# A fused decoder layer: when the second output projection begins, and where the down weights are split

## The chip, the cores and the metric

The kernel runs on one core of one Trainium2 chip. The metric is the device time of one execution in microseconds (us); lower is better. The core has five engines that run beside each other, each through its own list of instructions in a fixed order: TensorE (matmuls; PE in the profile, PEld for its weight loads), VectorE (DVE), ScalarE (ACT), GpSimd (POOL) and SyncE (SP, which here issues nearly all DMA transfers). An engine that waits for one instruction's inputs holds up all that stands behind it in its list.

## The reference

Two batches of 512 tokens of width 1024 go through one decoder layer with LayerNorm after each of three parts:

```python
x = layernorm(x + attn(x, wq, wk, wv, wo))        # 32 query heads, 8 key/value heads of 128,
                                                  # causal, window of 128 tokens
x = layernorm(x + matmul(fake_quant(x), fake_quant(ctx)))   # ctx: (2, 1024, 1024), 8-bit levels
x = layernorm(x + ffn(x, w_gate, w_up, w_down))   # silu(gate) * up, 2752 wide; both the inner
                                                  # values and the result are truncated to int8 steps
```

All inputs are float32. The truncations make the result depend on exact values, so the kernel keeps float32 precision where they lie.

## The kernel before, in words

Projections are computed with Strassen's scheme in the form with seven products: a product of a 2x2 block matrix takes seven block matmuls in place of eight, and sums of blocks on both sides are formed on VectorE. `strassen` (L119 to L174) emits the seven products of one weight tile, each of four matmuls into a PSUM bank, and yields after each. Its bank reads (L141 and L152 on ScalarE, L144, L155, L158, L161, L166, L169, L172 on VectorE) form the four blocks of the result.

**Attention** (`attention`) goes through 16 groups: eight key/value heads for each batch. For each group it projects keys, values and queries, and runs scores, softmax and the weighted sum (`scores`, `transpose_p`, `weigh`) in four blocks of 128 tokens. The sums of the attention output that the output projection needs are formed by `keep` and written to DRAM (`kept`, L422), seven slots for each group. The projections of a group are pieces of the group before; so in the last group of batch 1 (g = 7) there is no projection left to lie beside the softmax.

**The output projection** (`project_out`, L462 to L577) is a generator for each batch. It has 56 steps: seven products `k`, in the order of `grow`, times eight groups `g`. A step loads a right block of `wo` (or its precomputed sums) into `or`, a left tile `ol` from `kept`, forms sums of the right block on VectorE (`ot`, L500 to L505) and does seven matmuls (L560) into four PSUM banks `y`. After the eighth group of each product, `read(k)` (L532, L533) adds the banks into the residual tile `xres`. After products 5 and 3 two halves of the tokens are complete.

**The context part** (`Cross`): `context(b)` loads eight blocks of ctx (`raw`), quantises each with three VectorE operations (L612 to L618) and one on ScalarE, and sums columns with matmuls. `tokens(b)` takes a tile of 128 tokens through LayerNorm, quantise, transpose, matmul with the context (`m`, L683), LayerNorm again, and transpose into `x2T`, the input of the feed-forward part. Batch 0's tiles are written to DRAM (`spill`), as both batches use the same `xres` tile.

**The feed-forward part** (`feed_forward`) has 22 units for each batch: 21 of 128 rows of gate and up weights with `strassen`, and a rest of 64 rows. `activate` forms the inner values on ScalarE and VectorE. The down weights of a unit are loaded to `wd` (`load_down`, one buffer) and split into a high part `hi` (ScalarE, L762) and a low part `lo` (VectorE, L763) by `split`, so that two matmuls of a faster type give float32 accuracy. Every few units `down` (matmuls at L806) adds partial sums into `acc`. While batch 0's units run, the output projection, context and tokens of batch 1 are stepped in between.

**What sets the order.** The generators are stepped by three queues (`Background`). `behind` holds the context of batch 0 and both output projections; `aside` holds the tokens of batch 0, and then context and tokens of batch 1; `ahead` prepares weight sums. `in_attention` steps `behind` at each call and one other queue when the step was not a `LUMP`; `in_feed_forward` steps `aside` and `behind` once after each of the seven products of a unit. On top of this, the tile layer orders each engine's instructions by its own plan of when inputs are ready, so it may put an instruction ahead of others emitted earlier. `keep_in_program_order` marks an instruction that keeps its place in the emitted order on its engine. The order that comes out is fixed when the program is built.

Of the kernel before, what the change touches and what calls it, by code (L numbers as in the profile page):

```python
# [9 lines left out]
F32 = mybir.dt.float32  # L10
# [4 lines left out]
ALU = mybir.AluOpType  # L15
# [3 lines left out]
P = 128  # L19
# [3 lines left out]
D = 1024  # L23
# [155 lines left out]
class Background:  # L179
# [6 lines left out]
    def add(self, steps, share=1):  # L186

        self.queue.append([steps, share, 0])
# [273 lines left out]
def project_out(nc, tc, b, xres, spaces, psum, kept, complete, wo_d, sums, x_d, gap):  # L462
# [45 lines left out]
    while b and (b - 1, "tokens") not in complete:  # L508
        yield
# [5 lines left out]
    x = respool.tile([P, TPB, D], F32, tag="xres", name=f"xres{b}")  # L515
    for i in range(TPB):
        nc.sync.dma_start(out=x[:, i], in_=x_d[ts(b * TPB + i, P), :])
        xres[b * TPB + i] = x[:, i]
    yield
# [8 lines left out]
    def read(k):  # L528
        w = stream.tile([P, 4, HQ], F32, tag="right", name=f"yw_{b}_{k}")
        p1, u4, u2, u3 = (w[:, j] for j in range(4))  # L530
        q1, q6, q7, q5 = banks[0][:, 0], banks[0][:, 1], banks[1][:, 0], banks[3][:, 1]
        add = lambda out, in0, in1: nc.vector.tensor_tensor(out, in0, in1, ALU.add)  # L532
        nc.scalar.copy(p1, q1)  # L533
        tc.keep_in_program_order(add(u2, q6, p1))
        add(u3, q7, u2)
        add(u4, q5, u2)
        rows = w[:, 0:2], u3.unsqueeze(1).to_broadcast([P, 2, HQ])
        grown = banks[2], banks[3]
        to = [[x[:, 2 * h + q, ts(e, HALF)].rearrange("p (e c) -> p e c", e=2) for q in range(2)] for h, e in grow[k][1]]
        if len(to) == 1:  # L540
            for q in range(2):
                add(to[0][q], grown[q], to[0][q])
            for q in range(2):
                add(to[0][q], rows[q], to[0][q])
        else:
            whole = w[:, 0:2], w[:, 2:4]
            for q in range(2):
                add(whole[q], grown[q], rows[q])
            for block in to:
                for q in range(2):  # L550
                    add(block[q], whole[q], block[q])

    for n, (k, g) in enumerate(steps):
        while n + 2 < len(steps) and (b, steps[n + 2][1], "kept") not in complete:
            yield
        left, mine, sums_now = lefts.pop(n), factors.pop(n), following
# [15 lines left out]
        if g == LAST:  # L572
            read(k)
            if k in (5, 3):
                complete.add((b, 1 if k == 5 else 0))
            for j in range(gap):
                yield None if j else LUMP  # L577
# [137 lines left out]
def feed_forward(nc, tc, ident, xres, spill, x2T, xbuf, tpool, wpool, left, right, gate_up, wd_d, pools, stream, ps_y, out, between, finish_between):  # L715

    one_pool, raw_pool, b_work, ps_p = pools
    with ExitStack() as ctx:
# [18 lines left out]
        def load_down(u):  # L737
            m = units[u][1]
# [6 lines left out]
        def split(u):  # L745
# [16 lines left out]
            nc.scalar.copy(hi, raw[u])  # L762
            nc.vector.tensor_tensor(lo, raw[u], hi.bitcast(F32), ALU.subtract)  # L763
            halves[u] = (hi, lo)

# [73 lines left out]
        def finish(t, x, sums=None):  # L839

            if sums is None:
                sums = [acc[t]]
                a = wdp.tile([P, D], F32, tag="wd", name=f"fin_{t}", bufs=1)
# [53 lines left out]
        for u, (b, m) in enumerate(units):  # L897
            load_unit(u + 1)
            if m == NCHUNK:
                load_down(u)  # L900
            if m == NCHUNK:
                if b == 0:
                    finish_between()
                    right[1] = strassen_right(nc, tpool, x2T[1], "t2_1")
                rest_unit(u, b)
            else:
                g, up = gate_up_tiles(u)
                outs = g[:, :NH], g[:, NH:], up[:, :NH], up[:, NH:]
                for k, _ in enumerate(strassen(nc, (ps_p, ps_y if b else ps_p), work, left.pop(u), right[b], outs, u)):
# [4 lines left out]
                    if k == 1:  # L914
                        load_down(u)
                    between(k)
# [3 lines left out]
            split(u)  # L920
# [40 lines left out]
def decoder_layer(ctx, tc, x, xT, ctx_kv, wq, wk, wv, wo, s1, z1, s2, z2, wgu, wgu_rest, wd, out):  # L961
# [52 lines left out]
    def output(b):  # L1014
        return project_out(nc, tc, b, xres, (resid, stream), ps_y, kept[b], complete, wo, wo_sums, x, 2)
# [118 lines left out]

    aside.add(cross.context(1), 2)
# [52 lines left out]
```

## Time and profile before

| | us |
|---|---|
| median of three runs | 1926.13 |
| lowest, highest | 1924.7, 1931.46 |
| the profiled execution | 1926.28 |
| its span, first to last instruction | 1924.6 |
| PE busy in the span | 1879.7 |
| VectorE busy | 1369.9 |
| ScalarE busy | 562.5 |

The mean granted clock of TensorE over the span is 0.995 of full speed. The trace holds start and end of each instruction, what released it, and each DMA's issue and landing. Line numbers (L12) are those of the kernel before; tiles are named as in the program, without buffer numbers. In a row "1.66 <-ACT s L348" says that the engine stood idle for 1.66 us before the row's first instruction, and that it was released by ScalarE's instruction on tile `s` at L348. A float32 matmul shows as two records. In time on the span, attention of both batches takes 0 to about 1018 us, the feed-forward units of batch 0 about 1000 to 1550, those of batch 1 to about 1875, and the last sums, LayerNorms and output writes the rest.

### The profile page before, as it was taken

How to read it: one execution, taken by the hardware profiler on the slowest of the kernel's cores; microseconds unless marked ns; L12 is line 12 of the kernel's file. 1: busy time of each engine (PE TensorE's matmuls, PEld its weight loads, DVE VectorE, ACT ScalarE, POOL GpSimd, SP SyncE). 2: the span in 40 equal slices, each digit the busy share in tenths (PEclk: the TensorE clock that was granted, in tenths of full speed). 3: DMA queues.
4: the chain of work that ended last, by engine and by line, in shares of the span. 5: the costliest groups of instructions: out<-in, count | busy, mean ns of one | idle time of the engine just before them, and what ended most of it. 6: DMA issues, size and time to landing. Idle time of an engine off the chain costs nothing.

```text
span 1924.6 us, 24642 instructions
## 1 busy us (share of the span) xinstructions
PE 1879.7 (98%) x8666; PEld 1549.5 (81%) x8678; DVE 1369.9 (71%) x3021; ACT 562.5 (29%) x1569; POOL 13.7 (1%) x32
## 2 busy tenths in 40 slices
PE   9999999999999999999989999999999999999997
PEld 6888888888888888888767878888877778888885
DVE  4678888787767776777787876556778697555657
ACT  1333343333122122123452221111223354221224
POOL 0000000000000000000000000000000000000000
PEclk9999999999999999999989999999999999999999
DMA  8578788778798778855448765566653245543421
GB/s 306 176 264 288 275 279 281 259 258 265 242 328 269 264 273 294 279 171 199 154 169 317 274 226 188 206 225 205 211 193 119 83 168 188 185 169 119 150 97 44
DMA packets 183323, 416.88 MB, mean 217 GB/s; under 512 B 16672, under 2 KB 93728, under 8 KB 183200
## 3 DMA queue, kind: packets, MB, share of 16 engines
q1 hardware_dynamic: 181760, 412.94, 62.1%
q10 hardware_dynamic: 1440, 2.36, 0.3%
q8 instruction: 69, 1.13, 0.2%
q14 instruction: 54, 0.44, 0.1%
HBM read 318.77 MB, written 96.47 MB: 216 GB/s over the span
## 4 chain that ended last, share of the span: by engine, by line
PE 44%; DVE 9%; DMA 6%; ACT 3%; issue 1%; SPq 0%; DVEq 0%; ACTq 0%
PE prod L132 23%; PE y L560 11%; PE d L806 6%; DMA wd<-in_wd_dram 4%; DVE lo L763 1%; PE ps L336 1%; ACT hi L762 1%; PE m L683 1%; PE o L395 1%; PE o L396 1%; DMA raw<-in_ctx_dram 1%; PE x L692 0%; DVE halves L763 0%; PE rest L798 0%; PE pt L372 0%
## 5 line engine op out<-in xcount | busy, mean ns | idle before, releaser
L560 PE MATMUL y<-or,ol 128*128 128x256 f32 x896 | 246.4, 379 | 0.0
L560 PEld LDWEIGHTS y<-or,ol 128*128 128x128 f32 x896 | 168.9, 190 | 24.3 <-issue 1.0
L560 PE MATMUL y<-ot,ol 128*128 128x256 f32 x672 | 184.5, 383 | 3.9 <-DVE ot L501 3.2
L132 PE MATMUL prod<-xT,w 128*128 128x256 f32 x752 | 184.2, 381 | 0.2
L132 PE MATMUL prod<-t,w 128*128 128x256 f32 x752 | 177.2, 379 | 0.1
L132 PE MATMUL prod<-t,s 128*128 128x256 f32 x752 | 177.1, 379 | 0.1
L132 PE MATMUL prod<-x2T,wgu 128*128 128x256 f32 x672 | 162.5, 382 | 2.0 <-ACT st L141 2.0
L132 PEld LDWEIGHTS prod<-xT,w 128*128 128x128 f32 x752 | 139.6, 190 | 26.9 <-issue 9.6
L132 PEld LDWEIGHTS prod<-t,w 128*128 128x128 f32 x752 | 140.1, 190 | 24.3 <-issue 7.7
L132 PEld LDWEIGHTS prod<-t,s 128*128 128x128 f32 x752 | 140.3, 190 | 23.7 <-issue 5.3
L132 PE MATMUL prod<-t,wgu 128*128 128x256 f32 x672 | 157.3, 379 | 1.3 <-DVE st L144 1.3
L132 PE MATMUL prod<-t,sgu 128*128 128x256 f32 x672 | 156.9, 380 | 0.8 <-ACT x2T L693 0.8
L560 PEld LDWEIGHTS y<-ot,ol 128*128 128x128 f32 x672 | 125.1, 190 | 29.1 <-DVE ot L501 10.5
L132 PEld LDWEIGHTS prod<-x2T,wgu 128*128 128x128 f32 x672 | 128.2, 191 | 21.3 <-ACT st L141 2.8
L132 PEld LDWEIGHTS prod<-t,wgu 128*128 128x128 f32 x672 | 127.2, 190 | 20.3 <-DVE st L144 2.2
L132 PEld LDWEIGHTS prod<-t,sgu 128*128 128x128 f32 x672 | 126.9, 190 | 19.5 <-ACT x2T L693 1.6
L806 PE MATMUL d<-hi,act 128*128 128x512 f32 x256 | 108.1, 422 | 1.8 <-DMA or<-in_wo_dram 1.5
L360 ACT ACTIVATE s<-s,top 128x128 f32<-128x128 f32 x256 | 99.5, 390 | 33.8 <-DVE top L357 32.8
L346 ACT COPY s<-ps 128x128 f32<-128x128 f32 x192 | 39.6, 232 | 223.3 <-PE ps L336 223.3
L806 PE MATMUL d<-lo,act 128*128 128x512 f32 x256 | 101.1, 395 | 0.0
L820 DVE TENSOR_TENSOR acc<-d,acc 128x512 f32<-128x512 f32 x104 | 71.4, 690 | 41.3 <-PE d L806 40.8
L155 DVE TENSOR_TENSOR st<-prod,st 128x256 f32<-128x256 f32 x89 | 37.5, 422 | 84.2 <-PE prod L132 84.1
(210 smaller groups left out, 2985.8 us busy)
## 6 DMA issues: line engine op xcount, KB each, us to landing
kept<-factors SPq DMA_DIRECT2D x112, 448.0 KB, 3.6
ol<-kept SPq DMA_DIRECT2D x112, 448.0 KB, 5.1
w<-in_wq_dram SPq DMA_DIRECT2D x64, 512.0 KB, 4.4
or<-wo_sums SPq DMA_DIRECT2D x64, 512.0 KB, 5.1
sgu<-sums SPq DMA_DIRECT2D x42, 768.0 KB, 5.7
or<-in_wo_dram SPq DMA_DIRECT2D x48, 512.0 KB, 4.5
wgu<-in_wgu_dram SPq DMA_DIRECT2D x42, 512.0 KB, 4.2
wd<-in_wd_dram SPq DMA_DIRECT2D x42, 512.0 KB, 4.3
```

The source lines that it names most:

```text
L132: nc.tensor.matmul(ps, left[k - 1][:, c, :], right[k - 1][:, c, :], start=start and c == 0, stop=c == KH - 1, skip_group_check=True)
L155: nc.vector.tensor_tensor(u3, two, p1, ALU.add)
L336: nc.tensor.matmul(ps[:, k, cut // BLOCK : G + 1].rearrange("p d w -> p (d w)"), qT[b, g][:, G * i + c].rearrange("p h w -> p (h w)"), kT[ ...
L346: nc.scalar.copy(s[:, c, c * BLOCK :], ps[:, k, : G - c].rearrange("p d w -> p (d w)"))
L360: nc.scalar.activation(s[:, h, :], s[:, h, :], AF.Exp, bias=top[:, h : h + 1], scale=QSCALE, accum_out=total[:, h : h + 1],)
L395: nc.tensor.matmul(ps, v[b, g][:, i - 1, :], both, start=True, stop=False)
L396: nc.tensor.matmul(ps, vd[b, g][:, i - 1, :], cur, start=False, stop=True)
L560: nc.tensor.matmul(banks[bank][:, half], left[:, SLOT[j]], mine[j], start=grow[k][0] and g == 0 and half == 0, stop=g == LAST, skip_group_ ...
L683: nc.tensor.matmul(ps, a1T[:, c, :], a2[c][:, half], start=c == 0, stop=c == KC - 1)
L762: nc.scalar.copy(hi, raw[u])
L806: nc.tensor.matmul(ps, act[:, ts(i, P)], half[:, part], start=start and k == 0, stop=stop and k == len(parts) - 1)
L820: nc.vector.tensor_tensor(acc[t][:, ts(e, HALF)], ps, acc[t][:, ts(e, HALF)], ALU.add)
```

## The change

It has five parts.

1. The projection of batch 1 no longer waits at its beginning for the tokens of batch 0. It loads its first right and left tiles, then waits until the last group of attention has begun (`begun`, which is `last_group`). The tile `xres` of batch 1 is allocated and loaded at step 4 (`NKV - 4`), and only there does it wait for the tokens of batch 0.
2. `read(k)` is a generator: it forms all row sums first (`whole`), yields `LUMP`, adds the first block into `xres`, yields `LUMP` again, and adds the rest. The last add of each pair's first keeps its program order. The two yields that followed the read (`gap`) are gone.
3. The context of batch 1 is put behind 28 empty steps in `aside`, four units of seven.
4. For the units of batch 1, the down weight of the next unit is loaded after the fourth product of a unit (`k == 3`), and the split of the present one is made in two halves at fixed places: `hi` after the second product (`k == 1`), `lo` after the third (`k == 2`), both kept in program order. Before, load and split were emitted in the same unit and could be moved by the tile layer.
5. The working tile `fin` of the finish of batch 0's tokens moves from the tag `wd` to the tag `base`.

```diff
-def project_out(nc, tc, b, xres, spaces, psum, kept, complete, wo_d, sums, x_d, gap):
+def project_out(nc, tc, b, xres, spaces, psum, kept, complete, wo_d, sums, x_d, begun):
...
-    while b and (b - 1, "tokens") not in complete:
-        yield
     for n in range(3):
         load_right(n)
         if n < 2:
             load_left(n)
     yield
-    x = respool.tile([P, TPB, D], F32, tag="xres", name=f"xres{b}")
-    for i in range(TPB):
-        nc.sync.dma_start(out=x[:, i], in_=x_d[ts(b * TPB + i, P), :])
-        xres[b * TPB + i] = x[:, i]
-    yield
+    while b and not begun[0]:
+        yield
     following = right_sums(0)
...
-        to = [[x[:, 2 * h + q, ts(e, HALF)].rearrange("p (e c) -> p e c", e=2) for q in range(2)] for h, e in grow[k][1]]
-        if len(to) == 1:
+        whole = w[:, 0:2], w[:, 2:4]
+        for q in range(2):
+            add(whole[q], grown[q], rows[q])
+        yield LUMP
+        for n, (h, e) in enumerate(grow[k][1]):
             for q in range(2):
-                add(to[0][q], grown[q], to[0][q])
-            for q in range(2):
-                add(to[0][q], rows[q], to[0][q])
-        else:
-            whole = w[:, 0:2], w[:, 2:4]
-            for q in range(2):
-                add(whole[q], grown[q], rows[q])
-            for block in to:
-                for q in range(2):
-                    add(block[q], whole[q], block[q])
+                block = x[:, 2 * h + q, ts(e, HALF)].rearrange("p (e c) -> p e c", e=2)
+                last = add(block, whole[q], block)
+                if q == 0:
+                    tc.keep_in_program_order(last)
+            if n == 0:
+                yield LUMP
...
+        if n == NKV - 4:
+            while b and (b - 1, "tokens") not in complete:
+                yield
+            x = respool.tile([P, TPB, D], F32, tag="xres", name=f"xres{b}")
+            for i in range(TPB):
+                nc.sync.dma_start(out=x[:, i], in_=x_d[ts(b * TPB + i, P), :])
+                xres[b * TPB + i] = x[:, i]
...
         if g == LAST:
-            read(k)
+            yield from read(k)
             if k in (5, 3):
                 complete.add((b, 1 if k == 5 else 0))
-            for j in range(gap):
-                yield None if j else LUMP
...
         def load_down(u):
+            if u == len(units):
+                return
...
-            nc.scalar.copy(hi, raw[u])
-            nc.vector.tensor_tensor(lo, raw[u], hi.bitcast(F32), ALU.subtract)
+            first = nc.scalar.copy(hi, raw[u])
+            if u >= PER:
+                tc.keep_in_program_order(first)
             halves[u] = (hi, lo)
+
+        def rest_of_split(u):
+            hi, lo = halves[u]
+            last = nc.vector.tensor_tensor(lo, raw[u], hi.bitcast(F32), ALU.subtract)
+            if u >= PER:
+                tc.keep_in_program_order(last)
...
-                a = wdp.tile([P, D], F32, tag="wd", name=f"fin_{t}", bufs=1)
+                a = one_pool.tile([P, D], F32, tag="base", name=f"fin_{t}")
...
             if m == NCHUNK:
-                load_down(u)
-            if m == NCHUNK:
                 if b == 0:
+                    load_down(u)
                     finish_between()
                     right[1] = strassen_right(nc, tpool, x2T[1], "t2_1")
+                else:
+                    split(u)
+                    rest_of_split(u)
                 rest_unit(u, b)
...
-                    if k == 1:
+
+                    if b == 0 and k == 1:
                         load_down(u)
+                    elif b and k == 1:
+                        split(u)
+                    elif b and k == 2:
+                        rest_of_split(u)
+                    elif b and k == 3:
+                        load_down(u + 1)
                     between(k)
...
-            split(u)
+            if b == 0:
+                split(u)
+                rest_of_split(u)
+                if m == NCHUNK:
+                    load_down(u + 1)
...
+    aside.add(iter([None] * 28))
     aside.add(cross.context(1), 2)
     aside.add(cross_tokens(1))
```

More of the change, by code (lines that the diff above doesn't have):

```diff
@@ L1014, in output @@
     def output(b):
-        return project_out(nc, tc, b, xres, (resid, stream), ps_y, kept[b], complete, wo, wo_sums, x, 2)
+        return project_out(nc, tc, b, xres, (resid, stream), ps_y, kept[b], complete, wo, wo_sums, x, last_group)
     def cross_tokens(b):
```

## The prediction

> **What bounds the kernel now.** I read the page first, then busy time by stretch, then what TensorE waited for, then order and chain in the stretches that stand out.
>
> ```profile
> PE 1879.7 (98%) x8666; PEld 1549.5 (81%) x8678; DVE 1369.9 (71%) x3021; ACT 562.5 (29%) x1569; POOL 13.7 (1%) x32
> ```
>
> TensorE (PE) is the bound; nothing in the change removes one of its instructions, so all that can change is time in which it waits or runs slowly. By stretch (columns: length, busy us and count of PE, PEld, DVE, ACT, POOL, then granted clock, DMA share, GB/s):
>
> ```profile
> 970.00:985.00 15.00, 13.16 (x73) 10.11 (x73) 12.28 (x32) 12.78 (x38) 0.00 (x0) 1.00 0.49 160
> 985.00:1000.00 15.00, 10.65 (x45) 6.97 (x43) 12.41 (x28) 8.35 (x26) 0.00 (x0) 0.75 0.54 211
> 1000.00:1030.00 30.00, 28.09 (x115) 21.20 (x114) 19.83 (x46) 7.72 (x28) 0.00 (x0) 0.96 0.76 285
> 1030.00:1150.00 120.00, 116.19 (x525) 97.25 (x525) 93.74 (x185) 28.52 (x38) 0.00 (x0) 1.00 0.74 262
> 1150.00:1375.00 225.00, 225.00 (x1028) 192.94 (x1027) 139.37 (x291) 32.75 (x57) 0.00 (x0) 1.00 0.63 215
> 1375.00:1600.00 225.00, 219.06 (x995) 172.44 (x998) 178.27 (x370) 86.49 (x131) 1.94 (x3) 1.00 0.42 145
> 1600.00:1825.00 225.00, 219.24 (x991) 186.59 (x991) 133.06 (x226) 58.33 (x92) 0.95 (x1) 1.00 0.46 160
> ```
>
> Idle PE: 1.8+4.4+1.9 = 8.1 us from 970 to 1030 (end of attention, start of the feed-forward), 3.8 from 1030 to 1150, none from 1150 to 1375, 5.9 from 1375 to 1600 (tokens of batch 1 beside the feed-forward), 5.8 from 1600 to 1825 (second half of the feed-forward). These 23.6 us are what the change can reach. The order of PE's work in the first:
>
> ```profile
> 984.71 1.67 PE L683 MATMUL m<-a,a1T 128*128 128x512 bf16 x7 [1.66 <-ACT s L348]
> 993.00 1.44 PE L336 MATMUL ps<-kT,qT 128*128 128x160 f32 x4 [2.56 <-DVE s L350]
> 998.29 1.97 PE L692 MATMUL x<-ident,xres 128*128 128x128 f32 x8 [1.51 <-DVE xres L85]
> 1000.08 3.21 PE L132 MATMUL prod<-x2T,wgu 128*128 128x256 f32 x8
> ```
>
> PE waits for the last token tile of batch 0 (quantise, context product, LayerNorm, transpose) and for the last softmaxes, and there is nothing else in its order. It also slows: eight product records take 3.21 us here against 1.89 at 940 us, and the five groups from 993 to 1003 lose 0.73+0.49+0.70+0.94+1.32 = 4.2 us against the same groups elsewhere.
>
> What ended PE's waits, and in the last stretch the chain behind it:
>
> ```profile
> PE prod L132 <- DVE u L158: 5.8, 6, 1.4
> PE y L560 <- DVE ot L501: 3.2, 5, 1.7
> PE ps L336 <- DVE s L350: 3.2, 3, 2.6
> PE prod L132 <- ACT st L141: 2.0, 2, 1.5
> ...
> 1635.49 7.52 DMA wd<-in_wd_dram
> 1643.02 0.02 issue
> 1643.04 1.05 ACT hi L762
> 1644.10 0.02 issue
> 1644.12 1.22 DVE lo L763
> ```
>
> VectorE stands at a `lo` whose down weight has not landed, and behind it is the read of the product bank (L158) that PE needs. All six waits of 5.8 us lie between 1597 and 1809.
>
> **The change part by part.** The sum is against the profiled execution, 1926.3 us (span 1924.6); the median of three is 1926.1, the same.
>
> *Second output projection from the last group on.* In the changed kernel's instruction order 35 projection matmuls of batch 1 (all of the first five steps) stand ahead of the first feed-forward product; before, 10 do. A matmul is two records, eight records take 1.73 us, so one is 0.43 us and the 25 give 10.8 us of work in the hole; two attention products (four records of 0.43 us, 1.7 us) also come before it. Against this the chain grows. The context product `m` ends about 2.3 us later, as projections stand between its parts; the 20 further right sums on VectorE (0.34 us each start to start, 6.8 us) fall mostly into its 5.3 us of idle and the 2.3 us in which it waits for the square root (994.3 to 996.6). Followed by hand, x's transposes come at 1001.3 instead of 998.3 and the first product ends at 1006.6 instead of 1003.1: 10.8+1.7-3.5 = 9.0 us gained. One wait is new: step 7 of the projection now stands right behind the last attention product (about 1018), and needs factors of the last group that are written to DRAM (issued near 1010; the same write landed after 7.1 us before, beside four loads of x) and read back (4 to 5 us when quiet, 9 at the worst row): 1015 to 1023. I take 3 us there (0 to 6), and 1 us back from the slow matmuls. Hole: -7 us (-11 to 0).
>
> The row with the clock at 0.75 has no single wait over 2.56 us. The Trainium skill (TensorE: Matmul & The Clock Gate, Part 1) has the clock drop after an idle window of about 3.4 us; by that no wait here is long enough and the slow matmuls might stay in the changed kernel too, and the sum would be some 1 us less gain. The row shows the drop without such a wait, so I go by the row.
>
> *x of batch 1 loaded at step 4.* Four loads that wait for the spill of the last tile. SP stands 4.4 us for it (998.27 to 1002.69) in both; now projection loads for steps 4 to 8 are ahead of it in SP's order instead of behind, and only the last group's factor writes and step 7's load queue behind. That is the wait priced above.
>
> *Context put off by 28 steps.* Its eight blocks cost VectorE 0.81+0.69+0.69 = 2.2 us each, 17.5 us, and eight 512 KB loads. They go from 1010-1125 (VectorE 78% busy, 262 GB/s, 3.8 us of PE idle) to about 1110-1240 (62%, 215 GB/s, no idle). There SP passes weight and projection loads first. One block's late load (7.6 us to landing at 1116.9) made the 1.7 us wait at 1125; it can come again at another place. The lumps of the first read, in parts, stand between the activation's steps. Together -2.5 us (-4 to +2).
>
> *Read in parts.* Same count of VectorE operations: eleven for the first product, seven for the others. For single blocks the product banks are now read after the row sum instead of before it: about 0.3+3x0.42 = 1.6 us later on that bank, covered by two yields, each with four product matmuls (1.7 us). In attention it touches at most the 3.2 us of waits for `ot`: 0 (-2 to +2).
>
> *Tokens of batch 1.* Their order moves. From `m` to x's transposes VectorE and ScalarE need 9.9 us in the trace (988.4 to 998.3). In the new order the cover is 9.5 us or more for three tiles and 5.9 us for the last; between transpose and context product nine product matmuls stand for that tile where two stood. Of 5.9 idle and some 6 us of late issue I take -4 us (-8 to +4).
>
> *Split bound, weight loaded a unit ahead.* For batch 1, 22 units each have one ScalarE copy (1.05 us) and one VectorE subtraction (1.22 us) at a fixed place, in the first and second product of the unit, behind this order: `st` copy, `hi`, then the previous unit's magnitude. A unit is 28 matmuls, 12.1 us. The load goes out when `lo` ends, about 6 us into the unit, lands 3.1 to 7.5 us later (rows of this stretch), at 9 to 13.5, and is wanted at 14.4 (12.1 plus the first product). So the 5.8 us of waits behind `lo` go. Next late: the previous activation, 1.2 us longer. From L172 to its end took 6.1 us, so it ends 8.2 us into a unit where the bank read L155 is due at 8.7: 0.5 us spare, another 0.8 before PE stands. At the partial sums (one in four units) up to 0.5 us. -5 us (-6.5 to +3). `fin` moved to the `base` tile: its last readers are the tokens, done before; nothing waits.
>
> Sum: -7 -2.5 +0 -4 -5 = -18.5; 1926.3-18.5 = 1907.8, say **1908 us**. The tail after 1875 is unchanged.
>
> **The rivals.**
> *The wait only moves (not faster).* Step 7's factors come at 1023 or later, the softmax chain slips by the same, and the tokens give nothing: 0 -2.5 +0 +0 -5: 1918.8. For it: DMA at 285 GB/s after 1000, landings of 7 to 9 us there. Against: PE's order before step 7 has 4 us of attention waits of its own that hide part.
> The Trainium skill (DMA: Bandwidth & Descriptors, "Two DMAs through the same engine are not ordered") has the issuing engine wait for a write's semaphore before a read of the same bytes; that speaks against moving step 7 forward. Rows agree: loads of `ol` behind factor writes.
>
> *ScalarE stands at the bound copy (slower).* If a down weight lands later than 8.4 us after its issue, every unit of batch 1 loses the difference, as `hi` has a fixed place before the magnitude and the bank copies. With the other parts at -13.5 us, 20 units must lose 1.2 us each to reach +10: landing at 9.6 us, 1936 us. For it: all five loads of a unit now come in one burst. Against: the longest landing in this stretch is 7.5 us, a unit asks for 2.3 MB in 12.1 us, 190 GB/s.
>
> *All of it (faster yet).* Hole -11, context -4, tokens -8, splits -6.5: 1897.
>
> That the change is not made by the scheduler doesn't hold: the new order shows the moved matmuls and one split per unit.
>
> **How the numbers follow.** Forecast 0.62 (its own range 1901 to 1916), all of it 0.10, wait moves 0.16, ScalarE 0.12. Range 1896 to 1922: it reaches past 1897 and 1918.8 and leaves out the slower case. 0.5% is 9.6 us, about what a measurement of this kernel can tell from no change: faster 0.72, same 0.16, slower 0.12.
>
> **What would show it.** Right: PE over 13.5 of 15 us in the stretch before the first product with the clock near 1; the wait for `u` L158 under 1 us in total; no PE wait for a DMA over 3 us. Wrong: a PE wait for `ol` at step 7; ScalarE waiting for `wd` with PE idle behind it in batch 1; waits for `ot` or `st` grown between 1050 and 1550.

## The result, and the profile after

The changed kernel takes 1911.2 us (median of six runs, 1909.64 to 1915.19) against 1929.66 us for the kernel before on the same chip (1924.7 to 1931.99): ratio 0.991, 95% interval 0.9892 to 0.9929. The profiled execution took 1913.13 us with a span of 1911.1 us. The two profiled spans differ by 13.5 us and the medians by 18.5 us, because the profiled run of before (1926.28 us) is among its shorter ones and that of after among its longer ones. What follows accounts for the 13.5 us of the traces.

The page's line of engines, and busy time by stretch (columns: length, busy us and count of PE, PEld, DVE, ACT, POOL, then granted clock, DMA share, GB/s):

```profile
PE 1873.8 (98%) x8667; PEld 1552.2 (81%) x8678; DVE 1370.0 (72%) x3021; ACT 563.2 (29%) x1571; POOL 13.7 (1%) x32
```

```profile
970.00:985.00 15.00, 13.89 (x74) 10.47 (x73) 13.10 (x33) 9.19 (x28) 0.00 (x0) 1.00 0.71 231
985.00:1000.00 15.00, 12.17 (x51) 9.42 (x50) 12.96 (x34) 4.68 (x15) 0.00 (x0) 0.89 0.77 271
1000.00:1030.00 30.00, 27.96 (x127) 21.20 (x126) 20.49 (x43) 10.86 (x38) 0.00 (x0) 1.00 0.77 280
1030.00:1150.00 120.00, 119.40 (x543) 101.72 (x542) 85.09 (x169) 24.73 (x38) 0.00 (x0) 1.00 0.73 253
1150.00:1375.00 225.00, 222.68 (x1013) 189.41 (x1013) 152.56 (x316) 39.49 (x64) 0.00 (x0) 1.00 0.65 223
1375.00:1600.00 225.00, 216.09 (x982) 171.97 (x984) 174.69 (x361) 90.55 (x133) 1.93 (x3) 0.99 0.42 141
1600.00:1825.00 225.00, 224.55 (x1022) 193.36 (x1022) 129.70 (x223) 51.94 (x88) 0.00 (x0) 1.00 0.45 154
```

Set beside the same rows of before: the stretch from 985 to 1000 holds 51 matmul records in place of 45 and a clock of 0.89 in place of 0.75; from 1030 to 1150 PE is almost full (119.40 for 116.19); from 1150 to 1375 it has become less full (222.68 for 225.00), and so it has from 1375 to 1600 (216.09 for 219.06); from 1600 to 1825 it is full (224.55 for 219.24). The change wins in three places and loses in two. What PE waited for:

```profile
PE y L561 <- DMA ol<-kept: 4.1, 2, 2.8
PE x L691 <- DVE xres L85: 3.9, 1, 3.9
...
PE y L561 <- DVE ot L501: 2.9, 5, 1.6
```

The 5.8 us behind the bank read `u` L158 are gone. The two longest entries are new: a load of the projection that comes late, and the LayerNorm of batch 1's tokens.

Busy time alone misses what PE loses by running slowly, so I also took, for each matmul record of TensorE, the time from its start to the next matmul's start less the median of that for its tile and shape in the traces of before and after. A doubled interval within the products `m` or `cs` that shows no releaser counts as a missing record, and is no loss. In us lost, by stretch of the span, for all the kernels of this study ("rest" is from 1825 to the end; parts are numbered as in the change; part 5 goes with part 4, and is also in the row 1+2+3):

| kernel | 0–480 | 480–970 | 970–1030 | 1030–1150 | 1150–1375 | 1375–1600 | 1600–1825 | rest | sum |
|---|---|---|---|---|---|---|---|---|---|
| before | 7.7 | 9.2 | 14.9 | 5.7 | 1.2 | 12.1 | 7.6 | 3.7 | 62.1 |
| 1 | 6.8 | 8.4 | 8.3 | 11.4 | 1.2 | 11.2 | 7.5 | 3.7 | 58.5 |
| 4 | 7.2 | 10.5 | 14.2 | 7.4 | 1.8 | 12.6 | 1.2 | 3.7 | 58.5 |
| 1+4 | 6.9 | 10.8 | 8.0 | 9.3 | 1.3 | 11.3 | 1.2 | 3.7 | 52.5 |
| 2+4 | 7.7 | 11.5 | 17.9 | 4.8 | 2.2 | 15.0 | 1.7 | 4.0 | 64.9 |
| 3+4 | 6.4 | 10.1 | 15.2 | 3.3 | 4.3 | 12.0 | 1.2 | 3.7 | 56.2 |
| 2+3+4 | 7.5 | 10.9 | 16.2 | 1.7 | 5.9 | 14.6 | 1.6 | 3.7 | 62.1 |
| 1+3+4 | 7.0 | 11.3 | 7.9 | 2.6 | 3.7 | 10.9 | 1.0 | 4.1 | 48.4 |
| 1+2+4 | 7.7 | 5.4 | 8.3 | 6.6 | 1.2 | 16.0 | 1.2 | 3.7 | 50.1 |
| 1+2+3 | 7.2 | 5.7 | 6.9 | 2.7 | 3.1 | 15.2 | 8.2 | 3.7 | 52.7 |
| after (1+2+3+4) | 6.5 | 6.3 | 9.7 | 2.0 | 4.4 | 14.7 | 1.0 | 3.7 | 48.5 |
| after, batch 0's x early | 6.5 | 10.6 | 10.2 | 2.4 | 2.8 | 15.1 | 1.2 | 3.7 | 52.4 |
| after, batch 1 read whole | 6.3 | 6.4 | 8.8 | 2.6 | 6.8 | 11.4 | 1.3 | 3.7 | 47.3 |
| after, 56 steps | 7.4 | 5.3 | 6.3 | 0.6 | 7.3 | 14.4 | 0.9 | 3.7 | 45.9 |

The difference of the sums of before and after, 13.6 us, is that of the spans. Each row is one execution, so a single cell is good to perhaps 1 us (an estimate from the first column, which ranges over 1.4 us), and rows are compared column by column.

The end of attention in the changed kernel (the order of PE):

```profile
967.75 0.60 PE L691 MATMUL x<-ident,xres 128*128 128x128 f32 x4
...
990.63 0.71 PE L336 MATMUL ps<-kT,qT 128*128 128x160 f32 x4
994.17 2.08 PE L561 MATMUL y<-or,ol 128*128 128x256 f32 x4 [2.83 <-DMA ol<-kept]
...
1001.03 1.04 PE L691 MATMUL x<-ident,xres 128*128 128x128 f32 x8
...
1004.60 1.89 PE L132 MATMUL prod<-x2T,wgu 128*128 128x256 f32 x8
...
1019.34 1.10 PE L561 MATMUL y<-or,ol 128*128 128x256 f32 x4 [1.26 <-DMA ol<-kept]
```

The transposes come at 1001.03 us and the first product ends at 1006.5 us, where the order had said 1001.3 and 1006.6. That the times agree is partly luck, because this kernel reaches the hole early: the first transposes of the tile before the last stand at 967.75 us, where the kernel before has them 4 us later:

```profile
971.78 0.60 PE L692 MATMUL x<-ident,xres 128*128 128x128 f32 x4
```

From there to the last tile's transposes it takes 33.3 us, where before took 26.5 and the order followed by hand 29.5. The wait of step 7 is there, with 1.26 us. The larger wait, 2.83 us from 991.3 on, was not foreseen: the load of step 4's left tile, issued at 987.09 us among four other loads and a write, landed at 994.12 us.

### The profile page after: what moved, and what is told of

It reads as the page before. It is cut to its first block, busy times and chain, and to the rows that moved or that the text cites. A ratio compares the mean times of both kernels' runs of the same rounds, so it can differ in the third digit from the quotient of the medians.

```text
span 1911.1 us, 24650 instructions
## 1 busy us (share of the span) xinstructions
PE 1873.8 (98%) x8667; PEld 1552.2 (81%) x8678; DVE 1370.0 (72%) x3021; ACT 563.2 (29%) x1571; POOL 13.7 (1%) x32
## 4 chain that ended last, share of the span: by engine, by line
PE 81%; DVE 11%; DMA 3%; ACT 3%; issue 1%; SPq 0%; DVEq 0%; ACTq 0%
PE prod L132 47%; PE y L561 15%; PE d L814 7%; PE ps L336 3%; PE o L395 2%; PE o L396 2%; PE m L682 1%; PE pt L372 1%; DMA raw<-in_ctx_dram 1%; ACT s L360 1%; PE first L271 1%; DMA wd<-in_wd_dram 1%; DMA ol<-kept 1%; PE o L393 1%; DVE factors L407 0%
## 5 line engine op out<-in xcount | busy, mean ns | idle before, releaser
L561 PEld LDWEIGHTS y<-ot,ol 128*128 128x128 f32 x672 | 125.2, 191 | 27.6 <-DVE ot L501 7.6
```

The source lines that it names most:

```text
L561: nc.tensor.matmul(banks[bank][:, half], left[:, SLOT[j]], mine[j], start=grow[k][0] and g == 0 and half == 0, stop=g == LAST, skip_group_ ...
```

## The experiments

All were timed in five rounds beside the kernel before on the same chip; "before" in a ratio is that chip's.

**The first part undone.** The projection of batch 1 waits for the tokens of batch 0 at its beginning again, and both batches load x there.

```diff
+    while b and (b - 1, "tokens") not in complete:
+        yield
     for n in range(3):
         load_right(n)
...
+    x = respool.tile([P, TPB, D], F32, tag="xres", name=f"xres{b}")
...
-    while b and not begun[0]:
-        yield
...
-        if n == NKV - 4:
...
```

> The changed kernel with its first part undone: the projection of batch 1 again waits at its beginning for the tokens of batch 0, and loads x there. Everything else as changed. Theory (the 25 matmuls moved forward fill the hole at the end of attention): 6 to 9 us slower than the changed kernel (ratio to the kernel before about 0.995), and the granted clock near 0.75 again in the 15 us ahead of the first feed-forward product. Rival (the wait only moves, other parts carry the gain): within 2 us of the changed kernel, ratio 0.991 to 0.992.

Measured: 1928.7 us, ratio 0.9996 (0.9987 to 1.0004). All of the gain is gone, more than either theory allowed. The table's row 2+3+4 shows 6.5 us of it from 970 to 1030 and 4.6 us from 480 to 970. The granted clock from 985 to 1000 is 0.86, not the 0.75 that was expected, against 0.89 in the changed kernel; so the clock of this stretch does not tell the two theories apart. The edit also moves the loads of batch 0's x back, which a later run takes by itself.

**The fourth part undone.** Load and split of the down weights are free to move again.

```diff
-            first = nc.scalar.copy(hi, raw[u])
-            if u >= PER:
-                tc.keep_in_program_order(first)
+            nc.scalar.copy(hi, raw[u])
...
-                    if b == 0 and k == 1:
+                    if k == 1:
                         load_down(u)
-                    elif b and k == 1:
-                        split(u)
...
```

> The changed kernel with its fourth part undone: down weight loaded in its own unit, split emitted at the unit's end and free to be moved; the finish tile stays on the base tag. Theory (fixed places let the down weight land before VectorE reaches lo): 5 to 7 us slower than the changed kernel (ratio about 0.994), and 4 to 6 us of waits of PE for VectorE's L158 return in the units of batch 1. Rival (the waits went because the finish tile left the wd buffer): under 1 us of such waits, ratio 0.991.

Measured: 1918.47 us, 0.9956 (0.9944 to 0.9969), 7 us above the changed kernel by the medians and 9 by the ratios. In the waits of PE from 1600 to 1825 us of this run the read that stood behind `lo` is back:

```profile
PE prod L132 <- DVE u L158: 5.3, 5, 1.3
```

The tile `fin` is still on the tag `base` here, so the rival falls. Which half makes the gain, the load a unit earlier or the fixed places of the split, was not tried apart.

**The third part undone.** The context of batch 1 is queued without the 28 empty steps.

```diff
-    aside.add(iter([None] * 28))
     aside.add(cross.context(1), 2)
```

> The changed kernel without the 28 empty steps ahead of the context of batch 1. Theory of the prediction (the context is cheaper in the quieter stretch): 2 to 3 us slower than the changed kernel, ratio 0.992 to 0.993. Rival from the two traces (the waits of VectorE for late context blocks come wherever the context is; put off, they showed again near 1193 us and cost 4.5 us between 1163 and 1366): 0 to 4 us faster than the changed kernel, ratio 0.989 to 0.991.

Measured: 1913.12 us, 0.9926 (0.9911 to 0.9941), 2 to 3 us above the changed kernel, with intervals that overlap. By the table 4.6 us come back between 1030 and 1150 and 3.2 go between 1150 and 1375: the delay mostly moves the context's waits from one stretch to the next. The measured ratio fits the theory's range and lies just outside the rival's, but the place of the waits is as the rival had it.

**The second part undone.** `read` adds everything at once, and the two yields follow it again.

```diff
-        yield LUMP
-        for n, (h, e) in enumerate(grow[k][1]):
+            for block in to:
...
-            yield from read(k)
+            read(k)
...
+            for j in range(2):
+                yield None if j else LUMP
```

> The changed kernel with its second part undone: each read of the product banks is emitted at once, single blocks added from the banks first, and the two yields stand behind it. Theory of the prediction: within 2 us of the changed kernel, ratio 0.990 to 0.992. Rival (the 4.5 us that the changed kernel is ahead by the last group of attention come from reading in parts): 3 to 5 us slower, ratio 0.993, with waits of PE for the right sums back in attention, 3 us in total.

Measured: 1912.83 us, 0.9922 (0.991 to 0.9933), which can't be told from the changed kernel: the theory's total held. In the trace the sum does not move (48.4 for 48.5), but what it is made of does: reading in parts wins 5.0 us in attention from 480 to 970 and loses 3.8 us in the stretch of batch 1's tokens. The rival had the place in attention right; the waits for the right sums that it named come to 1.2 us there, not 3.

**Batch 0's x loaded at its beginning.** The changed kernel, in which batch 0's projection loads its x ahead of the first step, as before, and batch 1's at step 4. (The change puts the loads at step 4 in both batches, though it needs that only for batch 1.)

```diff
+    if b == 0:
+        x = respool.tile([P, TPB, D], F32, tag="xres", name=f"xres{b}")
...
+        yield
     while b and not begun[0]:
...
-        if n == NKV - 4:
+        if b and n == NKV - 4:
```

> The changed kernel, but batch 0 loads its x at the beginning of its projection again, with the yield behind it; batch 1 as changed. Question: why did undoing the first part cost 17 us and not 7, of which 4 to 5 us were already lost by the end of attention, before the projection of batch 1 has begun. Theory (the first part also takes one yield and four loads from the beginning of batch 0's projection, and this shifts its steps against the attention): 3 to 5 us slower than the changed kernel, ratio 0.993, all of it before the last group, waits of PE for the right sums back in attention. Rival (the loss in attention comes from the place of batch 1's loads in the queues): within 1.5 us of the changed kernel, ratio 0.991.

Measured: 1916.55 us, 0.9948 (0.9935 to 0.9962), some 7 us above the changed kernel by the ratios and 4 by the traces. The first load is issued at 27.6 us in place of 31.3, and none of the four shows a wait at either place. The edit also puts back a step, and with it shifts where the steps of batch 0's projection fall among those of attention. From 480 to 970 this run loses 10.6 us in place of 6.3. So the gain of the changed kernel in attention, which the prediction did not have, needs both the read in parts and batch 0's x at step 4. That this edit makes the difference was shown; that it does so through the interleaving, and not through the earlier loads, is my reading and was not tried apart.

**The split alone.** Before, with the fourth and fifth part.

```diff
-            nc.scalar.copy(hi, raw[u])
-            nc.vector.tensor_tensor(lo, raw[u], hi.bitcast(F32), ALU.subtract)
+            first = nc.scalar.copy(hi, raw[u])
+            if u >= PER:
+                tc.keep_in_program_order(first)
...
+                    elif b and k == 3:
+                        load_down(u + 1)
```

> The kernel before with only the fourth and fifth part of the change: the split bound, the down weight loaded a unit ahead, the finish tile on the base tag. Theory (its gain is its own, 5 to 7 us as undoing it cost 7): ratio 0.9965, and the waits of PE for VectorE's L158 under 1 us. Rival (the gain needs the other parts): ratio 0.999 to 1.000.

Measured: 1920.06 us, 0.9967 (0.9954 to 0.9979). 6.4 us without the other parts, 7 to 9 on top of them: this part's gain is its own. In the table it is the column from 1600 to 1825, 7.6 to 1.2, in every kernel that has it (0.9 to 1.7 us, against 7.5 to 8.2 without).

**In parts for batch 0, whole for batch 1.** If the read in parts wins in attention and loses in the tokens, the two ways together should keep the gain alone.

```diff
+        if b:
+            for block in to:
...
+            return
         whole = w[:, 0:2], w[:, 2:4]
...
+            if b:
+                yield LUMP
+                yield
```

> The changed kernel with the read in parts for batch 0 only; batch 1 reads at once, as before. From the run that read whole in both batches: it lost 5 us in attention and won about the same between 1420 and 1560 us, where the wait of PE for x's LayerNorm fell from 3.9 to 1.4 us. Theory (each effect belongs to its batch): 4 to 5 us faster than the changed kernel, ratio 0.9885. Rival (both effects come from the order of all instructions being planned anew, and do not add): within 2 us, ratio 0.990 to 0.992.

Measured: 1907.45 us, 0.9908 (0.9894 to 0.9923): not distinguishable from the changed kernel, so the rival held: the two effects do not add. In the table the tokens' stretch is 3.3 us better as meant, and the context's stretch ahead of it 2.4 us worse. Why the latter is so was not worked out.

**The first part alone.** Before, with the projection begun at the last group and x at step 4.

```diff
-    while b and (b - 1, "tokens") not in complete:
-        yield
...
+    while b and not begun[0]:
+        yield
...
+        if n == NKV - 4:
+            while b and (b - 1, "tokens") not in complete:
+                yield
```

> The kernel before with only the first part of the change: the projection of batch 1 begins with the last group, x loaded at step 4 in both batches. Theory (the hole is filled whatever the other parts do): 7 to 11 us faster than the kernel before, ratio 0.9945 to 0.9965. Rival (the first part is worth the 17 us that undoing it cost): ratio 0.991. Second rival (it needs the other parts, as the context of batch 1 then meets the first read): ratio over 0.998.

Measured: 1925.04 us, 0.9993 (0.9984 to 1.0002). The second rival held: alone it gives nothing that can be measured. Yet the hole is filled, 14.9 to 8.3 us in the table. The loss has gone to the first units of the feed-forward, where the context of batch 1 lies. PE's order there, and its busy time by stretch (columns as above), in this kernel:

```profile
1050.17 1.10 PE L562 MATMUL y<-or,ol 128*128 128x256 f32 x4 [1.09 <-DMA ol<-kept]
1053.17 0.76 PE L808 MATMUL d<-hi,act 128*128 128x512 f32 x1 [1.91 <-issue]
```

```profile
1045.00:1060.00 15.00, 11.21 (x35) 8.25 (x35) 11.95 (x24) 3.46 (x4) 0.00 (x0) 0.77 0.70 238
1060.00:1150.00 90.00, 88.10 (x396) 73.05 (x396) 66.32 (x132) 18.40 (x26) 0.00 (x0) 1.00 0.67 231
```

Loads of batch 1's projection, of its context and of a down weight are issued within 8 us there; a left tile comes late, 1.9 us more pass in a wait that the trace does not name, and the clock falls to 0.77. That the loads in common make the loss is my reading of these rows; no run tried it.

This left the question why undoing the first part costs 17 us when doing it alone gives one. The next three runs complete the set of the first three parts, always with the split bound.

**First part and split.**

```diff
+    while b and not begun[0]:
+        yield
...
+        if n == NKV - 4:
...
+            first = nc.scalar.copy(hi, raw[u])
+            if u >= PER:
+                tc.keep_in_program_order(first)
...
+                    elif b and k == 3:
+                        load_down(u + 1)
```

(the edits of "the split alone" and "the first part alone" together)

> Before with the first and the fourth part alone (projection begun with the last group, split bound in place); x is read as before, in one piece, and the second batch's context is not put off. The first part alone gave 0.9993 and the split alone 0.9967. If the parts simply add, this is 0.996 (some 7.5 us less than before). If the first part's gain only comes out together with the read in parts or the delay, and either of the two is enough (each left out of the changed kernel alone gave 0.9922 and 0.9926), it stays at 0.9955 to 0.997. Rival: the first part gives its 7 us as soon as the split is bound, and the other two are worth 1.5 to 3 us each: 0.992 to 0.994.

Measured: 1917.35 us, 0.9948 (0.9936 to 0.996), between the ranges of the two theories. The hole is filled (8.0 us lost, 14.2 with the split alone):

```profile
970.00:985.00 15.00, 14.88 (x73) 10.59 (x72) 11.72 (x28) 7.94 (x25) 0.00 (x0) 1.00 0.47 151
985.00:1000.00 15.00, 13.81 (x70) 10.64 (x69) 13.35 (x34) 5.65 (x22) 0.00 (x0) 1.00 0.93 334
1000.00:1030.00 30.00, 25.97 (x114) 18.87 (x112) 20.06 (x41) 11.71 (x39) 0.00 (x0) 1.00 0.70 263
```

**Delay and split.**

```diff
+    aside.add(iter([None] * 28))
     aside.add(cross.context(1), 2)
```

(on the kernel of "the split alone")

> Before with the third and the fourth part alone (28 empty steps ahead of the second batch's context, split bound in place). The split alone gave 0.9967; split, delay and read in parts together 0.9996, so that one of the latter two costs 5 us where the projection begins late. Theory: it is the delay, since the second batch's tokens then start later and nothing has been won ahead of them: 0.999 to 1.000. Rival: it is the read in parts, and the delay costs nothing here: 0.9955 to 0.9975.

Measured: 1922.62 us, 0.9972 (0.9961 to 0.9982). The rival held: the delay costs nothing here.

**Read in parts and split.** The kernel with the first part undone, and without the delay.

```diff
-    aside.add(iter([None] * 28))
     aside.add(cross.context(1), 2)
```

> Before with the second and the fourth part alone (x read in parts, split bound in place). Theory as of the delay with the split: the read in parts costs little where the projection begins late, 0.996 to 0.998. Rival: it is the read in parts that costs the 5 us, because its eight further operations of VectorE fall into the stretch in which the first feed-forward product waits for x: 0.999 to 1.001.

Measured: 1929.35 us, 1.0012 (1.0002 to 1.0022). The rival held: where the projection begins late, the read in parts costs 8.7 us ((1.0012-0.9967) x 1927), more than the 5 us expected. In the table, against the split alone, 3.7 us of it lie from 970 to 1030 and 2.4 us with the tokens of batch 1. PE's order in the hole of this kernel, and two of VectorE's LayerNorm rows:

```profile
984.78 0.63 PE L372 MATMUL pt<-ident,s 128*128 128x128 f32 x4 [3.31 <-DVE s L366]
...
996.44 1.09 PE L372 MATMUL pt<-ident,s 128*128 128x128 f32 x4 [3.43 <-DVE s L366]
...
1001.12 0.90 PE L336 MATMUL ps<-kT,qT 128*128 128x160 f32 x2 [2.52 <-DVE ln_c L66]
```

```profile
978.78 0.81 DVE L85 TENSOR_SCALAR xres<-xres,ln_mv,ln_r 128x1024 f32<-128x1024 f32 x1
...
1001.90 0.81 DVE L85 TENSOR_SCALAR xres<-xres,ln_mv,ln_r 128x1024 f32<-128x1024 f32 x1
```

The last LayerNorm of batch 0 comes at 1001.90 us here; in before it started at 997.4. PE's three waits of 9.3 us have no projection matmuls to lie beside. With the first part they have, and the same read in parts is then a gain.

**A longer delay.**

```diff
-    aside.add(iter([None] * 28))
+    aside.add(iter([None] * 56))
```

> The changed kernel with 56 empty steps instead of 28 ahead of the second batch's context. The profile of after loses 4.5 us between the units 5 and 9, where the context's matmuls wait for VectorE, and then 3.9 us at one wait for the second batch's x. Theory: the context's waits only move four units further and the second batch's x comes later: 0.991 to 0.994, no gain. Rival: the context falls clear of the second batch's projection and 3 us more are won: 0.989 to 0.990.

Measured: 1914.84 us, 0.9932 (0.9917 to 0.9947): no gain, as the first theory had it. In its trace the context's loss moves on from 1030–1150 (0.6 us) to 1150–1375 (7.3 us). The trace's sum is the lowest of all, but six runs from 1911.26 to 1918.25 do not bear it out. No version of this study is measurably faster than the changed kernel.

In shares of the time: with the split in, the first part is worth 0.19% alone (0.9967 to 0.9948), 0.50% with the delay (0.9972 to 0.9922), and 0.86% with the read in parts, with or without the delay (1.0012 to 0.9926, 0.9996 to 0.991). Without the split it is worth 0.07% (the first part alone). The read in parts costs 0.45% without the first part and wins 0.22% with it; where the delay is in, it is 0.24% and 0.12%. A ratio is good to some 0.13%, so a difference of two is good to some 0.18%. The 0.07% and 0.12% can't be told from nothing, and 0.19% to 0.24% only just can; from 0.45% on they stand well clear. The split is worth 0.33% alone, 0.45% on top of the first part and 0.46% on top of the first three. No other part has a price of its own.

Whether the wait for `ol` at step 4 goes away when left tiles are loaded three steps ahead was not tried.

## Why the prediction was right, and where its steps were not

The forecast was 1908 us and the median is 1911.2. The two mechanisms that carried most of the forecast, matmuls of the projection in the hole and the splits out of the way, are both in the trace. Point by point, in us of the traces:

| step | predicted | measured | by |
|---|---|---|---|
| hole | -7 | -5.2 (-6.5 by undoing) | column 970–1030 |
| context put off, first read | -2.5 | -0.5 | 1030–1150 (-3.7), 1150–1375 (+3.2) |
| read in parts, in attention | 0 | -4.1 (with batch 0's x at step 4) | 0–970 |
| tokens of batch 1 | -4 | +2.6 | 1375–1600 |
| split bound | -5 | -6.6 | 1600–1825 |
| sum | -18.5 | -13.8 | 13.6 but for rounding |

Against the profiled execution of after the forecast is 5 us low; against the median only 3, because the profiled run of after is among the longer ones. The terms miss by more than their sum does: two that failed by 2 and 6.6 us stand beside 4.1 us that the prediction did not have. So the near hit of the total is partly luck, and so is it that the medians differ by 18.5 us, the very sum that was forecast: by the traces it is 13.5, and the interval of the ratio is some 7 us wide.

The sum also prices each part as if it stood alone, and this assumption failed. The first part alone fills the hole (14.9 to 8.3 us lost) and gives nothing, because 5.7 us more are lost from 1030 to 1150. It pays only together with other parts.

**Hole: right, with one wait missed.** The order followed by hand came out within 0.3 us in the times on the span, but counted from the tile before it is 3.8 us too short (29.5 for 33.3), and the lead of 4 us out of attention hid that. The new wait for `ol` at step 7, put at 3 us, took 1.26. The step that failed was that step 7's load would be the only late one: step 4's took 7.0 us to land and cost 2.83 us. Together 4.1 us, one more than allowed. Of the 3.8 us, 2.83 pass in step 4's wait. The slow matmuls went only in part: the clock is 0.89 from 985 to 1000 where it was 0.75, and the last section shows behind which wait and why.

**Split: right, and a little small.** The reasoning on landings holds: in the changed kernel the 14 loads of `wd` from 1600 to 1825 us land after 3.1 to 4.5 us (median 3.4), inside the 3.1 to 7.5 that it used, while the stretch moves 154 GB/s and not the 190 that it worked out. ScalarE had stood 34.6 us at `hi` for these loads in before, in that stretch; in after no such wait is in its list.

**Context: the size failed.** The prediction counted on 38% idle VectorE and no idle PE from 1150 to 1375 to take the context without loss. Room on average was not room at each wait: the context's operations now lie there on VectorE (152.56 us busy for 139.37), and batch 1's projection waits for its sums `ot`, which VectorE also forms, for 2.3 us of the 4.4 lost. With 56 steps the same loss moved on with the context.

**Tokens of batch 1: the sign failed.** This is the term that was argued from the order's cover alone, 9.5 us of matmuls for three tiles. It left out that the read in parts puts the last adds of the projection into the tokens' way on VectorE. VectorE's order just ahead of the longest wait, then that wait:

```profile
1445.63 0.69 DVE L527 TENSOR_TENSOR xres<-yw,xres 128x512 f32<-128x512 f32 x1
1446.23 0.69 DVE L828 TENSOR_TENSOR acc<-d,acc 128x512 f32<-128x512 f32 x1
1446.83 0.68 DVE L527 TENSOR_TENSOR xres<-yw,xres 128x512 f32<-128x512 f32 x1
...
1450.94 1.21 DVE L770 TENSOR_TENSOR lo<-wd,hi 128x1024 fp32r<-128x1024 f32 x1
...
1452.89 0.81 DVE L85 TENSOR_SCALAR xres<-xres,ln_mv,ln_r 128x1024 f32<-128x1024 f32 x1
```

```profile
1453.76 1.25 PE L691 MATMUL x<-ident,xres 128*128 128x128 f32 x8 [3.86 <-DVE xres L85]
```

VectorE runs without a pause from the last adds to the LayerNorm, with the partial sums of `down` and the subtraction of a split between them. With batch 1's read whole, this wait is gone and the stretch loses 11.4 us, about before's 12.1: so the cost comes with the read in parts, as the table shows in every pair with and without it.

**Read in parts: zero in sum, but not by standing still.** It was costed at nothing with the waits for `ot` as its only reach; it wins 5 us in attention and gives 3.8 back with the tokens (after against 1+3+4). The step that failed is that it could touch only the waits for `ot`. Beside it, the prediction has no term for batch 0's x at step 4, and without that the gain in attention is gone (10.6 us lost for 6.3).

**The rivals.** "The wait only moves" fell: it put the hole's gain at 0, and the hole gained 5 to 6.5 us. "ScalarE stands at the bound copy" needed landings of 9.6 us; the longest was 4.5. "All of it" needed both the hole and the tokens to give more than they did. The signs named beforehand came out mixed: PE is busy 13.89 of 15 us from 970 to 985 but 12.17 from 985 to 1000, the wait for `u` is gone, no wait for a DMA in the changed stretches is over 2.83 us, and the wait for `ol` at step 7, named as a sign against, came without deciding anything. Of the last sign against, from 1050 to 1550 the waits for `ot` grew (1.7 to 2.9 us) and those for `st` fell (3.3 to 1.1).

What stays open: why attention loses 4 to 5 us less with just the pair of parts 1 and 2, beyond the fact; and the 1.9 us that the trace puts to no releaser in the first part alone.

## What to carry to other kernels

Where one engine is busy 98% of the span, a change that fills a hole is worth what the following stretches do not take back; here the projection begun early was worth 0.07% to 0.86% with 6.2 to 9.6 us won in the hole each time, by which other parts were in. Only the edit that took a late transfer out of an engine's fixed order (load a unit ahead, split at a fixed place) had a price that stayed much the same alone and together (0.33% to 0.46%), and that one could be predicted from rows. For the others, a stretch's average idle share says little: look at what stands in the waiting engine's queue just ahead of the instruction that is waited for.

## What the runs showed of the hardware

Whether the granted clock fell after a wait of TensorE was not decided by the length of the wait alone. Two kernels have one and the same wait of 3.31 us, for the softmax tile `s`. In the one with the read in parts and the split it is shown further up (the row at 984.78). In the one with the first part undone it is this:

```profile
983.68 0.63 PE L372 MATMUL pt<-ident,s 128*128 128x128 f32 x4 [3.31 <-DVE s L366]
```

After the wait at 984.78 the clock fell to 0.50; after the one at 983.68 it stayed at 1.00. What differs is where the wait lies on a grid of 3.41 us. In all traces of this study the granted clock is 1.00 or 0.50. The stretches at 0.50 that end within the span last 3.41, 6.83 or 10.24 us, and their edges in one trace lie whole multiples of 3.41 us apart: in the changed kernel they go from 993.76 to 997.17 and from 1454.56 to 1457.97, 135 steps of the grid later. On this grid (columns as above), first the read in parts and the split:

```profile
982.60:986.01 3.41, 1.23 (x12) 1.25 (x13) 2.24 (x7) 3.41 (x13) 0.00 (x0) 1.00 0.00 0
986.01:989.42 3.41, 3.41 (x14) 1.97 (x12) 3.41 (x7) 1.62 (x6) 0.00 (x0) 0.50 0.72 284
```

Then the first part undone:

```profile
978.80:982.21 3.41, 1.57 (x8) 0.85 (x6) 1.92 (x3) 3.38 (x10) 0.00 (x0) 1.00 0.50 190
982.21:985.63 3.42, 1.95 (x17) 1.76 (x18) 2.96 (x9) 3.42 (x15) 0.00 (x0) 1.00 0.00 0
```

Where the clock fell, most of the wait lies in one step of the grid, and 1.23 us of TensorE's work are left in that step. Where it stayed, two steps share the wait, with 1.57 and 1.95 us of work. The same count fits the wait for `ol` at step 4, which is 2.83 us in the changed kernel and 1.77 us with 56 empty steps; the changed kernel first:

```profile
990.35:993.76 3.41, 0.98 (x7) 0.69 (x5) 3.15 (x10) 2.97 (x10) 0.00 (x0) 1.00 1.01 368
993.76:997.17 3.41, 3.00 (x9) 2.54 (x10) 2.70 (x12) 0.54 (x4) 0.00 (x0) 0.50 0.61 249
```

```profile
991.60:995.01 3.41, 1.83 (x10) 1.64 (x11) 3.15 (x10) 2.76 (x11) 0.00 (x0) 1.00 1.02 407
995.01:998.43 3.42, 3.42 (x19) 3.07 (x19) 3.42 (x13) 0.65 (x2) 0.00 (x0) 1.00 0.71 221
```

It also fits the two waits of 1.09 and 1.91 us in the first part alone: the step from 1049.10 to 1052.52 has 1.10 us of work, and the clock is 0.50 from 1052.52 to 1059.35. In the fourteen traces, from 10 to 1890 us, each of the sixteen steps at full clock with under 1.4 us of work is followed by 0.50, and none with over 1.8 us is; between the two both occur. The Trainium skill (TensorE: Matmul & The Clock Gate, Part 1) has the clock drop after an idle window of about 3.4 us; here a step of that length was enough though it held 0.98 us of work, so for a stretch such as this one the measurement decides. A wait of 2 to 3 us can thus cost more than its length, 9 matmul records in the 3.41 us behind it against 19 where the clock stayed, and whether it does depends on where it falls.
